# Four-layer graph network on one core: layer 0 and layer 2 sum the normed inputs, weights go to the sums or into the gates, x and out lie partition-major, and the first loads come in another order

## The chip, the cores and the metric

The kernel runs on one core of a Trainium2 chip. The metric is device time in microseconds (us), the median of several runs. One execution was taken by the hardware profiler; its page and its trace are what the text calls the profile. Engines: PE is TensorE (matmuls; PEld its weight loads), DVE is VectorE, ACT is ScalarE, POOL is GpSimd, SP is SyncE.

## The reference, cut to what matters

The input x has 4096 rows of 64 numbers, adj is a 4096 x 4096 matrix of zeros and ones (0.8% ones). Each of four layers norms x per row, applies relu, runs a graph operation with adj, and adds the result to x.

```python
h = relu(layernorm(x))
# layer 0: w is a matrix of decaying powers of 0.5, from a running count of each row's ones
x = x + (w @ (h @ L0_weight) + L0_bias)
# layer 1: attention, masked by adj, on Lorentz-projected h; then x = x + support / norm
# layer 2: two gated steps, each
m = adj @ (g @ W)
gi = m @ wih.T + bih
gh = g @ whh.T + bhh
r = sigmoid(i_r + h_r); z = sigmoid(i_z + h_z); n = tanh(i_n + r * h_n)
g = relu((1 - z) * n + z * g)
# layer 3: weighted midpoint in hyperbolic space: adj @ (gamma * XW), adj @ (gamma - 1), row sums
```

Since matrix products associate, `w @ (h @ W)` is `(w @ h) @ W`, and `(adj @ (g @ W)) @ wih.T` is `(adj @ g) @ (W @ wih.T)`. The change uses both.

## The kernel before, in words

Rows are kept in 32 blocks of 128; block b, partition p, is row 128 b + p. Four quarters of 8 blocks (`q`) are the unit of most vector work: a tile of 128 partitions x 8 blocks x 64 features, 512 numbers to a partition. The adjacency is read once, transposed, as 128 tiles of 128 x 1024 numbers (quarter of columns q, block of rows b), and cast to fp8 on the way by GpSimd's queue (`load0`, L1084 to L1089); it stays on the chip. The same matrix is read a second time as it is, in 128 f32 tiles named `whole`, by the sync queue (`checks`, L1049), only to check that every entry is 0 or 1; VectorE does that in whatever gaps it has. A flag from it chooses a general path, which isn't taken here.

Layer 0 (`stream0`, L1091) walks over the tiles. For each, matmuls with two triangular matrices (`ftri`, `fupd`) keep a running count in PSUM (`cnt`); ScalarE or VectorE turns the count into a power of two (`w`), and two steps later `sums` multiplies `w` with the source. A source in f32 is split by `split3` into three bf16 parts, `hm` (two parts, 128 columns) and `lo` (one, 64 columns), so that bf16 matmuls add up to f32 accuracy. Before the change the source is `h @ w0`: `pre0` norms a quarter of x (`relu_ln`), transposes it on PE (`transpose4`, tile `ps_t`), multiplies it by the weights (`linear4`, tile `ps_l`) and splits. After the sums of a quarter, `post0` takes them from PSUM (`evac`), adds the bias there, transposes them back (`to_nm`, tile `ps_n`), adds them to x and goes on to `pre1`, the projections of layer 1.

Layer 1 (`stream1`) computes scores, a sigmoid, a mask and f32 sums. Then `post1` ends with `source2`: transpose the normed input g, send the transposed copy to memory (`g_spill`), multiply it by W (`linear4`), split. Layer 2 (`layer2`, two steps) sums fp8 adj with these sources; `load2` brings the spilled copy back beside the sums; `gates` multiplies sums and copy by the gate weights in one matmul of 128 rows (64 for the sums, 64 for the copy), four gate columns per parity of the column block; `post2a` makes the second step's source from the result, again with `source2`. Layer 3 (`layer3`) sums a 196-column source, and `post3` writes out.

Nothing of this order is left to the hardware. A planner (`Weave`) runs when the program is built: it keeps a clock for each engine from estimated costs, and a piece of vector work (a generator) is put into the program where its estimated start fits. `weave.work` is served first, two pieces at a time (`width`), `weave.back` (the checks) last. `land` estimates when a transfer arrives, one after another at 1.45 us for an adjacency tile. `until` puts pending work into the program until a named source is done. Each engine then runs its own list in order, and a wait stops what stands behind it.

At the start, the sync queue loads four quarters of x, ScalarE's queue the constants W (553 KB), and GpSimd first builds the identity and an index pattern, then loads A tiles. x is loaded a second time in layer 0, quarter by quarter, for the residual sum. In memory x is by rows, so a quarter comes in pieces of 64 numbers (256 B); so does out.

Of the kernel before, what the change touches and what calls it, by code (L numbers as in the profile page):

```python
# [18 lines left out]
P = 128  # L19
# [16 lines left out]
def general_kernel(ctx: ExitStack, tc: tile.TileContext, t: dict, out: bass.AP):  # L36
# [50 lines left out]
    x_nm = t["x"].rearrange("(b p) d -> p b d", p=P)  # L87
# [438 lines left out]
    out_nm = out.rearrange("(b p) d -> p b d", p=P)  # L526
# [54 lines left out]
class Layout:  # L581


    def __init__(self):
        self.n = 0
        self.at = {}
        for name, width in (("w0", 2 * D), ("w1", 2 * D), ("wkq", 4 * D), ("gw1", 2 * D), ("gw2", 2 * D),
                            ("w3", 2 * D), ("b1", D), ("bkq", 2 * D), ("b0", 1), ("gb1", 6), ("gb2", 6),
                            ("scales", 5), ("g1", 8 * D), ("g2", 8 * D)):
            self.at[name] = slice(self.n, self.n + width)  # L590
            self.n += width
# [200 lines left out]
def fast_kernel(ctx: ExitStack, tc: tile.TileContext, t: dict, out: bass.AP, flag: bass.AP):  # L792
# [47 lines left out]

    W = const.tile([P, L.at["scales"].stop], F32, name="W")
    x_nm = t["x"].rearrange("(b p) d -> p b d", p=P)
    xq = {}

    def load_x(q):
        xq[q] = b2(f"x{q}")
        Y_.dma_start(xq[q], x_nm[:, q * QB:(q + 1) * QB, :])
        weave.at[xq[q].tensor.name] = 6.0 + 1.0 * (NQ - 1 - q), "S"

    for q in range(NQ)[::-1]:  # L850
        load_x(q)
    S_.dma_start(W, t["consts"][:, :L.at["scales"].stop])
# [17 lines left out]
    S_.activation(es, w("scales", 0, 3), AF.Exp)  # L870
    att_mul = const.tile([P, 1], F32, name="fatt_mul")
    V.reciprocal(att_mul, w("scales", 4, 5))
    V.tensor_scalar(att_mul, att_mul, 2.0, None, op0=ALU.mult)
    att_add = const.tile([P, 1], F32, name="fatt_add")
    V.tensor_tensor(att_add, att_mul, w("scales", 3, 4), ALU.add)
    gate_b = const.tile([P, 4], F32, name="gate_b")
    for i in (1, 2):
        V.tensor_tensor(gate_b[:, 2 * i - 2:2 * i], w(f"gb{i}", 0, 2), w(f"gb{i}", 3, 5), ALU.add)


    A8 = [[const.tile([P, 2, 2 * CW], F8, name=f"A{q}_{i}") for i in range(NB // 2)] for q in range(NQ)]
# [5 lines left out]
    def squares(v, nb=QB):  # L887

        sq = b2("sq")[:, :nb, :v.shape[2]]
        yield AC.activation(sq, v, AF.Square)  # L890
        s = stat("ss", nb)
        yield DV.tensor_reduce(s, sq, AX.X, ALU.add)
        return s
# [23 lines left out]
    def relu_ln(x, dst):  # L917

        m = stat("mean", QB)
        yield DV.tensor_reduce(m, x, AX.X, ALU.add)  # L920
        xc = b2("xc")
        yield DV.scalar_tensor_tensor(xc, rows(m), -1.0 / D, x, op0=ALU.mult, op1=ALU.add)
        v = yield from squares(xc)
        yield DV.tensor_scalar(v, v, 1.0 / D, LN_EPS, op0=ALU.mult, op1=ALU.add)
        r = yield from rsqrt(v)
        yield DV.scalar_tensor_tensor(dst, xc, 0.0, rows(r), op0=ALU.max, op1=ALU.mult)
# [48 lines left out]
    def split3(ps, scale, hm, lo):  # L975

        yield AC.activation(hm[:, :, :D], ps, AF.Copy, scale=scale)
        r = b2("rest")
        yield DV.scalar_tensor_tensor(r, ps, scale, hm[:, :, :D], op0=ALU.mult, op1=ALU.subtract)
        free(ps)  # L980
        yield AC.activation(hm[:, :, D:], r, AF.Copy)
        yield DV.tensor_tensor(lo, r, hm[:, :, D:], ALU.subtract)
# [5 lines left out]
    def parts(layer, q):  # L988
        HM[layer, q] = b2(f"hm{layer}_{q}", (P, QB, 2 * D), BF16)
        LO[layer, q] = b1p.tile([P, QB, D], BF16, tag="b1", name=f"lo{layer}_{q}")  # L990
        return HM[layer, q], LO[layer, q]
# [4 lines left out]
    def add_hm(acc, layer, b, c, rhs, first, last=False):  # L996
        o = like(acc[c], rhs)
        mm(o, HM[layer, b // QB][:, b % QB, :], rhs, start=first, stop=last)

    def add_lo(acc, layer, b, c, rhs, last):  # L1000
        o = like(acc[c], rhs)[c * D:(c + 1) * D]
        mm(o, LO[layer, b // QB][:, b % QB, :], rhs, start=False, stop=last)

    def evac(acc, bias=None):

        lo, hi = slice(0, D), slice(D, P)
        a, mt = b2("agg", (P, CW)), b2("mt", (P, CW))
        sides = ((lo, hi), (hi, lo))
        for ps, (own, other) in zip(acc, sides):
            yield AC.activation(mt[own, :], ps[other, :], AF.Copy)  # L1010
        for ps, (own, other) in zip(acc, sides):
            if bias is None:
                yield DV.tensor_tensor(a[own, :], ps[own, :], mt[own, :], ALU.add)
            else:
                yield DV.scalar_tensor_tensor(a[own, :], ps[own, :], bias[own, :], mt[own, :],
                                              op0=ALU.add, op1=ALU.add)
            free(ps)
        return a
# [17 lines left out]
    def pre0(q):  # L1036
        h = b2("h0")
        yield from relu_ln(xq[q], h)
        fm = b2("h0T", (P, CW))
        yield from transpose4(h, 1, fm)  # L1040
        yield from split3(blocks((yield from linear4(fm, w("w0"), 1))), W0, *parts(0, q))
        DONE.add((0, q))
# [39 lines left out]
    tiles = [(q, b) for q in range(NQ) for b in range(NB)[::-1]]  # L1082

    def load0(n):  # L1084

        if n < len(tiles):
            q, b = tiles[n]
            weave.land(A8[q][b // 2].tensor.name, 1.45)
            nc.gpsimd.dma_start(A8[q][b // 2][:, b % 2, :], adjT[b * P:(b + 1) * P, q * 2 * CW:(q + 1) * 2 * CW])  # L1089

    def stream0():  # L1091
# [4 lines left out]
        def turn(q, b):  # L1096

            n = q * NB + NB - 1 - b
            a = a8(q, b)
            wt = b2("w", (P, 2 * CW), I16)  # L1100
            for c in (0, 1):
                if b < NB - 1:
                    before = a8(q, b + 1)(c)
                    mm(like(cnt[c], before), upd, before, start=False, stop=False)
                mm(like(cnt[c], a(c)), tri, a(c), start=b == NB - 1, stop=b == 0)

                if c == 0 or b % 2 == 0:
                    S_.activation(wt[:, cols[c]], cnt[c], AF.Relu, scale=-128.0)
                else:
                    V.tensor_scalar(wt[:, cols[c]], cnt[c], -128.0, 0.0, op0=ALU.mult, op1=ALU.max)  # L1110
            load0(n + 12)
            return [wt[:, x].bitcast(BF16) for x in cols]
# [20 lines left out]
        def here(item):  # L1133
            part = 0, item[1] // QB
            return part in DONE and weave.ready("P", names(LO[part])) <= weave.t["P"]

        for q in range(NQ):
            cnt[:] = [two(f"cnt{c}")[:, :CW] for c in (0, 1)]
            for b in range(1, NB, 2)[::-1]:

                if len(waiting) > 3:
                    weave.until((0, waiting[0][1] // QB), DONE)
# [11 lines left out]
                waiting.append((q, b, w0, w1))  # L1154
                if len(waiting) > 2 and here(waiting[0]):
                    for _ in sums():
                        weave.draw()
                if b == NB // 2 + 1:
                    xq[q] = b2(f"x{q}")
                    Y_.dma_start(xq[q], x_nm[:, q * QB:(q + 1) * QB, :])  # L1160
# [15 lines left out]
    def post0(q, acc):  # L1176
        X = xq.pop(q)
        a = yield from evac(acc, w("b0"))
        ps = yield from to_nm(a, 1)
# [146 lines left out]
    def post1(q, acc, kind):  # L1326
# [20 lines left out]
        yield from relu_ln(X[q], g)  # L1347
        gT = b2("gT", (P, CW))
        yield from transpose4(g, kind, gT)
        yield from source2(q, 0, gT, kind)  # L1350
# [4 lines left out]
    def source2(q, step, gT, kind):  # L1355
        g_spill[step, q] = dram.tile([P, CW], F32, name=f"gs{step}_{q}")
        yield AC.dma_start(g_spill[step, q], gT)
        ps = yield from linear4(gT, w(f"gw{step + 1}"), kind)
        yield from split3(blocks(ps), 1.0, *parts(2 + step, q))
        DONE.add((2 + step, q))  # L1360
# [36 lines left out]
    def layer2(step, post):  # L1397
# [11 lines left out]
        for q in range(NQ):  # L1409
            load2(step, q)  # L1410
# [19 lines left out]

    def gates(q, step):
# [4 lines left out]
        rz, ih = [None], [None]  # L1436

# [26 lines left out]
    def post2a(q):  # L1464
        x = yield from gates(q, 0)
        yield AC.activation(x, x, AF.Relu)
        yield from source2(q, 1, x, 1 if q < NQ - 1 else 2)
# [108 lines left out]
    out_nm = out.rearrange("(b p) d -> p b d", p=P)  # L1576
# [59 lines left out]
    out_nm = out.rearrange("(b p) d -> p b d", p=P)  # L1636
# [66 lines left out]
    weave.dma = 5.2  # L1703
    for n in range(12):
        load0(n)
    for q in range(NQ)[::-1]:
        weave.add(pre0(q))
# [4 lines left out]
    gate_w = []  # L1712
    for step in range(2):
        gate_w.append(b2(f"g{step}", (P, 8 * D)))
        Y_.dma_start(gate_w[step], t["consts"][:, L.at[f"g{step + 1}"]])
# [5 lines left out]
def pack_consts(given):  # L1721
# [20 lines left out]
    for r in (0, D):  # L1742
        put("b0", given("L0_gnn_bias").reshape(D, 1), r)
    for i, name in enumerate(("scale", "scale_q", "scale_k", "att_bias", "att_scale")):
        put("scales", np.broadcast_to(given("L1_gnn_" + name).reshape(1, 1), (P, 1)), 0, i)
    for i in (1, 2):
        diag(f"gw{i}", given(f"L2_gnn_W{i}"))
        ih, hh = given(f"L2_gnn_wih{i}").T, given(f"L2_gnn_whh{i}").T
        for par in range(2):
            x, m = (0, D) if par == 0 else (D, 0)  # L1750
            for g, (wm, wx) in enumerate(((0, 0), (1, 1), (None, 2), (2, None))):
                col = (4 * par + g) * D
                if wm is not None:
                    put(f"g{i}", ih[:, wm * D:(wm + 1) * D], m, col)
                if wx is not None:
                    put(f"g{i}", hh[:, wx * D:(wx + 1) * D], x, col)
# [52 lines left out]
```

## Time and profile before

| | |
|---|---|
| Time, median of 3 runs | 824.69 us (824.64 to 824.71) |
| Span of the profiled run | 823.2 us |
| PE, DVE, ACT, POOL busy | 786.9, 625.3, 398.0, 69.8 us |
| First matmul starts | 7.97 us |
| First sum of layer 0 (`acc`) | 21.98 us |
| First score of layer 1 | 239.88 us |
| Last matmul ends | 802.5 us |
| DMA packets, of these under 512 B | 56,499 and 17,648 |

Busy is the time in which an engine had work in hand; matmuls are pipelined, so a busy PE is not PE at its peak. The chain of work that ended last is followed back from the last instruction, at each step to what released it. A wait is put down to the engine or transfer that came last.

### The profile page before, as it was taken

How to read it: one execution, taken by the hardware profiler on the slowest of the kernel's cores; microseconds unless marked ns; L12 is line 12 of the kernel's file. 1: busy time of each engine (PE TensorE's matmuls, PEld its weight loads, DVE VectorE, ACT ScalarE, POOL GpSimd, SP SyncE). 2: the span in 40 equal slices, each digit the busy share in tenths (PEclk: the TensorE clock that was granted, in tenths of full speed). 3: DMA queues.
4: the chain of work that ended last, by engine and by line, in shares of the span. 5: the costliest groups of instructions: out<-in, count | busy, mean ns of one | idle time of the engine just before them, and what ended most of it. 6: DMA issues, size and time to landing. Idle time of an engine off the chain costs nothing.

```text
span 823.2 us, 12224 instructions
## 1 busy us (share of the span) xinstructions
PE 786.9 (96%) x4570; PEld 367.6 (45%) x4570; DVE 625.3 (76%) x1393; ACT 398.0 (48%) x607; POOL 69.8 (8%) x143
## 2 busy tenths in 40 slices
PE   5989999999999999999999999999999999999990
PEld 2433444443433333333333333444444444699990
DVE  6565666676567888888888878978789787775896
ACT  5646556556565567666666663022210244452323
POOL 4322324323000000000000000000000000000000
PEclk9999999999999999999999999999999999999995
DMA  9999999999901023022022025796879900000010
GB/s 134 113 235 221 156 220 115 175 200 156 203 21 40 1 91 114 1 89 65 1 89 65 1 70 198 270 340 214 277 248 349 322 15 14 1 2 2 2 40 17
DMA packets 56499, 100.54 MB, mean 122 GB/s; under 512 B 17648, under 2 KB 34032, under 8 KB 56432
## 3 DMA queue, kind: packets, MB, share of 16 engines
q1 hardware_dynamic: 36128, 79.18, 29.1%
q0 software_dynamic: 18432, 16.79, 21.7%
q10 hardware_dynamic: 1872, 3.71, 1.2%
q8 instruction: 38, 0.62, 0.3%
q14 instruction: 29, 0.24, 0.1%
HBM read 144.75 MB, written 5.24 MB: 182 GB/s over the span
## 4 chain that ended last, share of the span: by engine, by line
PE 86%; DVE 7%; DMA 3%; ACT 2%; issue 1%; SPq 0%; POOL 0%; DVEq 0%; ACTq 0%; POOLq 0%
PE acc L940 52%; PE score L940 13%; PE cnt L940 12%; DMA whole<-in_adjT 3%; PE ps_l L940 2%; PE rz L940 2%; DVE sig L781 2%; PE ps_t L944 2%; PE ih L940 1%; DMA A<-in_adjT 1%; DVE ss L781 1%; PE ps_kq L940 1%; DVE nt L781 1%; ACT sig L781 1%; PE ps_n L944 0%
## 5 line engine op out<-in xcount | busy, mean ns | idle before, releaser
L781 ACT ACTIVATE sig<-score,fatt_add,fatt_mul 128x1024 f32<-128x1024 f32 x128 | 148.0, 1201 | 83.0 <-PE score L940 80.8
L781 DVE TENSOR_TENSOR sig<-sig,A 128x1024 f32<-128x1024 f32 x128 | 151.4, 1222 | 35.9 <-ACT sig L781 35.2
L781 DVE SCALAR_TENSOR_TENSOR whole<-whole 128x1024 f32<-128x1024 f32 x128 | 153.1, 1219 | 9.5 <-DMA whole<-in_adjT 8.7
L781 ACT ACTIVATE w<-cnt 128x512 int16<-128x512 f32 x192 | 108.4, 595 | 91.4 <-PE cnt L940 90.2
L940 PE MATMUL score<-qd,kT 64*128 64x512 f32 x512 | 128.0, 616 | 0.0
L940 PE MATMUL acc<-sig,S 128*64 128x512 f32 x512 | 125.4, 606 | 1.7 <-DVE sig L781 1.6
L940 PE MATMUL acc<-A,hm 128*128 128x512 fp8e4 x512 | 115.9, 379 | 0.8 <-DVE X L781 0.8
L940 PEld LDWEIGHTS <-hm 128*128 128x128 bf16 x768 | 73.2, 98 | 91.1 <-issue 12.6
L940 PE MATMUL cnt<-A,ftri 128*128 128x512 fp8e4 x256 | 97.8, 385 | 8.0 <-DMA A<-in_adjT 8.0
L940 PE MATMUL cnt<-A,fupd 128*128 128x512 fp8e4 x248 | 95.4, 385 | 4.6 <-DVE w L781 3.0
L940 PE MATMUL acc<-S,A 128*128 128x196 bf16 x1024 | 88.3, 247 | 0.0
L940 PEld LDWEIGHTS <-A 128*128 128x128 fp8e4 x1024 | 87.2, 97 | 1.1 <-issue 0.8
L781 DVE TENSOR_SCALAR w<-cnt 128x512 int16<-128x512 f32 x64 | 44.2, 691 | 54.7 <-PE cnt L940 51.5
L1089 POOL DMA_DIRECT2D A<-in_adjT x128 | 68.0, 533 | 141.4 <-DMA A<-in_adjT 136.9
L940 PEld LDWEIGHTS score<-qd,kT 64*128 64x128 f32 x512 | 43.8, 186 | 79.8 <-ACT sig L781 35.3
L940 PE MATMUL acc<-w,hm 128*128 128x512 bf16 x256 | 75.5, 379 | 0.0
L940 PEld LDWEIGHTS acc<-sig,S 128*64 128x64 f32 x512 | 30.4, 136 | 81.1 <-issue 38.5
L940 PEld LDWEIGHTS <-lo 128*64 128x64 bf16 x768 | 36.8, 109 | 58.2 <-issue 36.5
L940 PE MATMUL acc<-A,lo 128*64 128x512 fp8e4 x512 | 59.3, 380 | 0.0
L781 ACT ACTIVATE mt<-acc 64x512 f32<-64x512 f32 x32 | 18.9, 592 | 64.7 <-PE acc L940 64.1
L1565 POOL MEMSET S<- 128x4 bf16 x8 | 0.9, 116 | 529.3 <-PE ps_l L940 484.0
L940 PEld LDWEIGHTS <-fupd 128*128 128x128 bf16 x248 | 24.3, 98 | 44.5 <-issue 22.3
(176 smaller groups left out, 652.8 us busy)
## 6 DMA issues: line engine op xcount, KB each, us to landing
whole<-in_adjT SPq DMA_DIRECT2D x128, 512.0 KB, 6.8
A<-in_adjT POOLq DMA_DIRECT2D x128, 128.0 KB, 12.4
x<-in_x SPq DMA_DIRECT2D x8, 256.0 KB, 15.5
qd<-qs SPq DMA_DIRECT2D x16, 128.0 KB, 4.5
mx<-gs SPq DMA_DIRECT2D x16, 128.0 KB, 8.1
xT<-gs SPq DMA_DIRECT2D x8, 256.0 KB, 7.5
xs<-x SPq DMA_DIRECT2D x4, 256.0 KB, 5.9
qs<-qT ACTq DMA_DIRECT2D x4, 256.0 KB, 6.1
```

Of the source, the lines that this page charges most:

```text
L781: return fn(*args, **kw)
L940: nc.tensor.matmul(o, lhsT, rhs, start=start, stop=stop, skip_group_check=True)
L944: nc.tensor.transpose(o, src, ident)
L1089: nc.gpsimd.dma_start(A8[q][b // 2][:, b % 2, :], adjT[b * P:(b + 1) * P, q * 2 * CW:(q + 1) * 2 * CW])
L1565: nc.gpsimd.memset(S3[q, c][:, :, 3 * e:], 1.0)
```

## The change

The change does four things. Layer 0 takes `h` itself as source; `post0` multiplies the sums by `w0` (`linear4` in place of `to_nm`), and the bias is added to x. Layer 2 takes g itself as source; its W is multiplied into the gate weights on the chip, once per step (`load_gates`: one f32 matmul of 192 columns, four copies into the gate matrix), and the transposed copy is spilled after the split. x and out lie in memory as partition x block x feature, arranged on the host, so that a quarter is 2 KB to a partition. And the first loads are reordered: A, x, A, x ahead of the identity; quarters 1 and 0 of x and the constants during the stream, the last on ScalarE's queue; the last quarter's first norm in two halves; its vector work and that of the next quarter on VectorE alone, and the first 12 tiles' `w` on ScalarE alone. It is meant to take matmuls off TensorE and to start the stream earlier.

```diff
-    x_nm = t["x"].rearrange("(b p) d -> p b d", p=P)
+    x_nm = t["x"]
...
-    for q in range(NQ)[::-1]:
-        load_x(q)
-    S_.dma_start(W, t["consts"][:, :L.at["scales"].stop])
+    weave.dma = 1.0
+    load0(0)
+    load_x(3, Y_)
+    load0(1)
+    load_x(2, Y_)
...
-    def pre0(q):
-        h = b2("h0")
-        yield from relu_ln(xq[q], h)
-        fm = b2("h0T", (P, CW))
-        yield from transpose4(h, 1, fm)
-        yield from split3(blocks((yield from linear4(fm, w("w0"), 1))), W0, *parts(0, q))
-        DONE.add((0, q))
+    def pre0(q, c=None):
+        x = xq[q] if c is None else xq[q][:, c * CB:(c + 1) * CB]
+        h = b2("h0")[:, :x.shape[1]]
+        dve = q > 1
+        yield from relu_ln(x, h, dve)
+        yield from split3(h, W0, *parts(0, q, c), psum=False, dve=dve)
+        DONE.add((0, q) if c is None else (0, q, c))
...
-                if c == 0 or b % 2 == 0:
+                if c == 0 or b % 2 == 0 or n < 12:
                     S_.activation(wt[:, cols[c]], cnt[c], AF.Relu, scale=-128.0)
...
+                if q == 0 and b in (NB - 1, NB - 3):
+                    load_x((b - NB + 3) // 2, S_)
+                    weave.add(pre0((b - NB + 3) // 2))
+                if q == 0 and b == NB - 9:
+                    S_.dma_start(W, t["consts"][:, :L.at["scales"].stop])
+                    weave.add(constants())
...
-        a = yield from evac(acc, w("b0"))
-        ps = yield from to_nm(a, 1)
+        yield DV.tensor_tensor(X, X, w("b0")[:, None, :].to_broadcast([P, QB, D]), ALU.add)
+        a = yield from evac(acc)
+        ps = blocks((yield from linear4(a, w("w0"), 1)))
...
+        yield from split3(g, 1.0, *parts(2, q), psum=False)
+        DONE.add((2, q))
         gT = b2("gT", (P, CW))
         yield from transpose4(g, kind, gT)
-        yield from source2(q, 0, gT, kind)
+        yield from spill2(q, 0, gT)
...
-        ps = yield from linear4(gT, w(f"gw{step + 1}"), kind)
-        yield from split3(blocks(ps), 1.0, *parts(2 + step, q))
-        DONE.add((2 + step, q))
+        DONE.add(("spill", step, q))
...
+    def load_gates(step):
+
+        g, m = b2(f"g{step}", (P, 8 * D)), b2(f"m{step}", (P, 5 * D))
...
+            ps = two("ps_g")
+            mm(ps[:, :3 * D], m[:, :2 * D], m[:, 2 * D:])
...
-        yield from source2(q, 1, x, 1 if q < NQ - 1 else 2)
+        ps = yield from to_nm(x, 1 if q < NQ - 1 else 2)
+        yield from split3(ps, 1.0, *parts(3, q))
+        DONE.add((3, q))
+        yield from spill2(q, 1, x)
...
-    for q in range(NQ)[::-1]:
-        weave.add(pre0(q))
+    for c in (1, 0):
+        weave.add(pre0(NQ - 1, c))
+    weave.add(pre0(NQ - 2))
```

## The prediction, made before the change was run

> **What bounds the kernel now.** I read the page's busy times and the chain first, then the groups, then 5 us stretches and the timeline of the first 25 us, then TensorE's waits. The page:
>
> ```profile
> PE 786.9 (96%) x4570; PEld 367.6 (45%) x4570; DVE 625.3 (76%) x1393; ACT 398.0 (48%) x607; POOL 69.8 (8%) x143
> ...
> PE 86%; DVE 7%; DMA 3%; ACT 2%; issue 1%; SPq 0%; POOL 0%; DVEq 0%; ACTq 0%; POOLq 0%
> ```
>
> TensorE (PE) is 86% of the chain that ended last, and its idle time is 823.2 - 786.9 = 36 us. Most of that lies at the ends: 8 us before the first matmul, and 21 us after the last (802.5 to 823.2), where VectorE works through layer 3's last sums. So a matmul taken away between 22 and 800 us should show in the end, and one put in should cost. The stretches of the start say where else PE idles (columns: length, then PE, PEld, DVE, ACT, POOL busy, clock, DMA share, GB/s):
>
> ```profile
> 0.00:5.00 5.00, 0.00 (x0) 0.10 (x1) 0.72 (x3) 1.28 (x1) 4.39 (x14) 1.00 0.57 173
> 5.00:10.00 5.00, 1.77 (x4) 0.51 (x4) 4.32 (x17) 1.43 (x3) 1.71 (x4) 1.00 1.16 137
> ...
> 45.00:50.00 5.00, 4.13 (x24) 2.04 (x23) 1.88 (x4) 2.58 (x6) 1.06 (x2) 1.00 1.08 254
> 50.00:55.00 5.00, 3.62 (x22) 1.67 (x21) 3.64 (x6) 2.28 (x4) 1.06 (x2) 1.00 1.08 256
> ```
>
> The DMA engines are full from 5 us on (share above 1), and there is a hole of 2.3 us between 45 and 55 us. PE's waits in the first 60 us:
>
> ```profile
> PE cnt L940 <- DMA A<-in_adjT: 8.0, 1, 8.0
> PE cnt L940 <- DVE w L781: 2.8, 3, 1.5
> PE cnt L940 <- ACT w L781: 0.8, 3, 0.3
> ```
>
> The first wait is for the first adjacency tile, which shares the DMA engines with four loads of x and 553 KB of constants. The second is VectorE stuck on a check of the adjacency (`whole`) whose transfer, issued at 30.6, was queued behind a load of x and landed only at 47.4. The rows that I price with:
>
> ```profile
> L940 PE MATMUL ps_l<-W,h0T 128*128 128x128 f32 x32 | 4.2, 275 | 0.0
> L944 PE MATMUL ps_n<-fident,agg 128*128 128x128 f32 x32 | 5.0, 280 | 0.0
> L940 PE MATMUL ps_kq<-W,hlT 128*128 128x256 f32 x32 | 8.4, 386 | 0.0
> x<-in_x SPq DMA_DIRECT2D x8, 256.0 KB, 15.5
> A<-in_adjT POOLq DMA_DIRECT2D x128, 128.0 KB, 12.4
> ```
>
> Means of pipelined matmuls overlap, so I take a group's cost from the chain, where a piece runs to the next start: four transposes 0.44 us, one `linear4` 0.89 us (1.09 where it follows the half-array matmuls of layer 1).
>
> [...] `cnt` matmuls start at 9.62, 10.05, 10.47, then from 13.08 every 0.215 us. About 10 cold matmuls cost 10 x 0.21 = 2.1 us[...]. [...] x in rows of 64 floats is 256 B, 1024 packets a load, and its median landing is 15.5 us, while a 512 KB `whole` tile takes 6.8. [...] DMA shares above 1 agree that the engines are the limit. [...] the trace has 20 at 1283.
>
> **Part by part.**
>
> (a) Layer 0 sums `h` and not `h @ w0`. `pre0` loses four transposes and a `linear4`: 4 x (0.44 + 0.89) = 5.3 us of PE, and a ScalarE copy (0.59) each. `post0` pays for it: `linear4` in place of `to_nm`, 4 x (0.89 - 0.44) = +1.8 us. The bias becomes one VectorE add of 0.69 us per quarter on x, issued before the sums are evacuated, so it lies beside the end of the sums: zero. Net PE -3.5 us.
>
> (b) Layer 2, first step: `linear4` goes. On the chain its four read 1.09, 1.09, 1.09 and 0.89, so -4.2 us. The first three lie inside layer 1, which PE bounds (10.0 busy of each 10 us from 300 to 480). The fourth is on the 12 us way from the last `ps_n` (505) to the source of the last quarter; PE has the sums of other blocks there, so only its own time counts.
>
> (c) Layer 2, second step: `linear4` becomes four transposes, 3.8 - 2.0 = -1.8 us. The spill to memory now follows the split in place of leading it, and the reload waits for it; the reload of quarter 0 comes after the source of quarter 3 is done, some 20 us later, and the mx and xT loads land in 8 us. Hidden by the block sums.
>
> (d) Weights folded on the chip: one f32 matmul of 192 columns per step, by the 256-column row (0.43 us a matmul in the chain) 0.33 each, +0.65 us, plus four short ScalarE copies of half height and 160 KB of extra load each, beside PE. They need a two-bank PSUM tile, which at 500 us is free. Bounds 0.4 to 1.5; I take 0.7.
>
> (e) First loads. The first A tile goes out ahead of everything, with only one x load beside it. Before, it was issued at 1.46 and the first matmul came at 7.97. Lower bound of the new landing: issue at about 0.5 plus 3.7 (the shortest landing of a 512 KB tile) = 4.2; upper bound: 0.5 plus 6.5, the shortest A landing so far, = 7.0. The triangle matrices are ready at 2.3 now and perhaps 3.3 after, so they hide. I take 5.0: -3 us. Will PE then have work? Tiles arrive every 1.25 to 1.45 us (spacing of the POOL issues, without and with x beside them); a cold tile costs 4 x 0.43 = 1.7, so supply holds through the warm-up. The sums begin when the split of the last blocks is done: x lands at about 4, then 8 VectorE operations on 256 elements (0.42) and 9 small ones (0.2) make 5.2 us, so 9.5 to 12 us, where before the first sum stood at 21.98. From then PE has 3.25 us of work for each pair of tiles against 2.9 at most of supply.
>
> All of it on VectorE is three chains, 5.2 + 5.2 + 7.5 = 18 us in the first 22, which is why `w` goes to ScalarE alone for 12 tiles: 1.2 us a tile, less than the supply takes. It fits, narrowly.
>
> (f) Constants come mid-stream: the Exp now needs a table load at about 20 us, 1.28 us of ScalarE while PE waits for its `w`. Bounds 0 and 1.3; I take +0.6.
>
> (g) x and out by partition: 2 KB pieces for 256 B. In layer 0 a load of x holds the A spacing at 1.45 for some 10 us where it is 1.25 without, and `whole` tiles queue behind it on the sync queue. I expect half of the 5 us of waits described below to go: -2.5. At the end the last store issues at 817.75 and the span ends 5.4 us later; fewer packets may save 0.3.
>
> **The sum.** Layer 0 up to the first score (239.9 us): 64 pairs of `cnt` at 1.83, 62 of sums at 1.42, 5.3 of `pre0` and 3 x 4.8 of `post0` and `pre1` are 225 us; the other 15 are 8 of start, 2 cold, 5 of waits. After: 225 - 5.3 + 3 x 0.45 = 221; lost 5.0 + 2.1 + 1 (until the sums run) + 2.5 + 0.6 = 11.2; together 232.2, so -7.7. The fourth `linear4` of `post0` stands in layer 1: +0.45. Layer 2: -4.2 - 1.8 + 0.7 = -5.3. End: -0.3. Total -12.8: 824.7 - 12.8 = 811.9, say 812.
>
> **The rivals.**
> Work only: the first tile lands hardly earlier, or the VectorE chains delay the sums, and a new wait replaces the old ones. Then (a) to (d) remain, about -9, less 1 for (f): 816.5. For it: the full DMA and VectorE's 18 us in 22.
> More: the hole at 45 to 55 us and the later waits on `w` go wholly, since no x blocks the queue, and the tile lands at 4.2: 2.5 + 1 + 0.8 more: 807.5. For it: all those waits trace to slow transfers.
> Slower: the schedule is planned from costs, and a shorter layer 0 holds fewer checks (10 us less at 1.4 each, some 8). They go to layer 2, where VectorE is full in several stretches (5.00 of 5 from 525), and what is left is put in one run ahead of layer 3's evacuations, which free PSUM: 8 x 2 us = 16, against 12.8 gained: 828. Against it: VectorE has 10 us of 15 free at 750 to 765.
> No change: the same with half that pile, 824.
>
> **How the numbers follow.** Forecast 0.58, work only 0.2, more 0.12, no change 0.04, slower 0.06. The range 806.5 to 818.5 takes in the first three with (d) to (g) at their bounds. Faster 0.90, same 0.04, slower 0.06.
>
> **What would show it.** First matmul at 4.2 to 7; first `acc` sum at 10 to 14; first score near 232; no `ps_l` from gT or xT; `ps_l` from agg in place of one `ps_n`; packets under 512 B down from 17,648 by the 8 x 1024 of x and the 4096 of out, to some 5,400; PE busy down by about 8 us. The forecast fails if PE shows a new wait on `w` in the first 25 us, if `whole` tiles stand in the last 60 us before the end with PE idle, or if A tiles come late between 25 and 80 us.

## The result, and the profile after

| | before | after |
|---|---|---|
| Time, median | 824.7 us (824.64 to 825.05) | 832.87 us (830.46 to 833.05) |
| Ratio, 95% interval | | 1.0091 (1.0073 to 1.011) |
| Span of the profiled run | 823.2 us | 831.3 us |
| First matmul, first sum of layer 0 | 7.97, 21.98 us | 7.10, 14.66 us |
| Last matmul ends | 802.5 us | 797.7 us |
| Packets under 512 B | 17,648 | 5,392 |

The change made the kernel slower by 0.9%, where 1.5% faster was forecast. The profiled run is the longest of the four. The page of the changed kernel, busy times and chain:

```profile
PE 780.2 (94%) x4494; PEld 358.9 (43%) x4494; DVE 629.2 (76%) x1415; ACT 396.7 (48%) x611; POOL 69.7 (8%) x143
...
PE 83%; DVE 8%; DMA 5%; issue 1%; ACT 1%; POOL 0%; DVEq 0%; ACTq 0%; POOLq 0%
```

TensorE (PE) has 6.7 us less to do, nearly the 8 forecast, and its last matmul ends 4.8 us earlier. Yet the span ends 8.1 us later: the tail behind the last matmul grew from 20.7 to 33.6 us, and the chain lies 8% on VectorE (DVE) in place of 7% of a shorter span. Cut by stage, from the first and last instruction of each group of matmuls (the last column is a run told below):

| us | before | forecast | after | both causes mended |
|---|---|---|---|---|
| start to first score | 239.8 | 232.2 | 234.3 | 234.2 |
| first to last score (layer 1) | 257.5 | 254.7 | 258.4 | 254.8 |
| last score to first layer-3 sum | 210.8 | 208.8 | 208.7 | 206.8 |
| first layer-3 sum to end | 115.1 | 114.8 | 129.9 | 116.3 |
| sum | 823.2 | 810.5 | 831.3 | 812.1 |

The forecast column takes the prediction's terms into their stages: 257.5 + 0.45 - 3 x 1.09, and 210.8 - 0.89 - 1.8 + 0.7. Layer 2 came out as forecast. Three stages did not, the last of them by 15 us. Each column is one profile. In the first row a difference of 1 us means little: the changed kernel's start is the same in nine of the runs told below, and there its first matmul stands at 6.1 to 6.9 us and not at 7.10, its first sum at 13.4 to 13.9 and not at 14.66; in the four of them that have the same layer 0 too, the first score comes at 233.1 to 233.6. VectorE's timeline of the changed kernel there (start, length, engine, line, operation, and in brackets the idle time before it and what ended it):

```profile
757.99 0.89 DVE L781 TENSOR_TENSOR n<-n,acc 128x260 f32<-128x260 f32 x2 [2.21 <-ACT alpha L781]
758.79 1.22 DVE L781 SCALAR_TENSOR_TENSOR whole<-whole 128x1024 f32<-128x1024 f32 x1
...
771.97 1.23 DVE L781 SCALAR_TENSOR_TENSOR whole<-whole 128x1024 f32<-128x1024 f32 x1 [0.61 <-DMA whole<-in_adjT]
...
773.23 1.23 DVE L781 SCALAR_TENSOR_TENSOR whole<-whole 128x1024 f32<-128x1024 f32 x1
...
774.78 0.62 DVE L781 TENSOR_TENSOR n<-n,acc 128x130 f32<-128x130 f32 x2
```

Between two pieces of layer 3's work on the sums stand twelve checks of the adjacency (`whole`), from 758.79 to 774.50, three of the last four waiting for their loads too (1.3 us together). They are the checks that found no gap in the earlier layers; `layer3` issues all that are left in one run, behind the sums of its second set. Before the change one check stood there. The tile `whole` from 740 us on, in the kernel before and in the changed one:

```profile
L781 DVE SCALAR_TENSOR_TENSOR whole<-whole x1: 1218/1218/1218, 765.5 to 765.5; 128x1024 f32<-128x1024 f32 x1
```
```profile
L781 DVE SCALAR_TENSOR_TENSOR whole<-whole x12: 1217/1218/1226, 758.8 to 773.2; 128x1024 f32<-128x1024 f32 x12
```

Stretches of the kernel before around its one check (columns: length, then PE, PEld, DVE, ACT, POOL busy, clock, DMA share, GB/s):

```profile
750.00:755.00 5.00, 5.00 (x62) 5.00 (x60) 0.88 (x3) 0.50 (x2) 0.00 (x0) 1.00 0.00 0
755.00:760.00 5.00, 5.00 (x62) 5.00 (x60) 1.16 (x4) 0.68 (x4) 0.00 (x0) 1.00 0.02 3
760.00:765.00 5.00, 5.00 (x61) 5.00 (x60) 1.48 (x5) 1.13 (x6) 0.00 (x0) 1.00 0.00 0
765.00:770.00 5.00, 5.00 (x61) 4.80 (x59) 4.76 (x17) 0.80 (x3) 0.00 (x0) 1.00 0.01 3
770.00:780.00 10.00, 10.00 (x121) 10.00 (x119) 9.14 (x46) 4.32 (x14) 0.00 (x0) 1.00 0.01 2
```

and of the changed kernel around the run and behind it:

```profile
745.00:750.00 5.00, 5.00 (x62) 5.00 (x60) 0.00 (x0) 0.00 (x0) 0.00 (x0) 1.00 0.00 0
750.00:755.00 5.00, 5.00 (x61) 5.00 (x60) 1.75 (x6) 1.24 (x8) 0.00 (x0) 1.00 0.00 0
755.00:758.80 3.80, 3.80 (x47) 3.80 (x46) 1.36 (x5) 0.57 (x4) 0.00 (x0) 1.00 0.02 4
758.80:774.50 15.70, 14.98 (x177) 14.75 (x174) 14.26 (x26) 1.02 (x6) 0.00 (x0) 1.00 0.60 202
...
780.00:790.00 10.00, 10.00 (x121) 10.00 (x119) 8.78 (x40) 3.31 (x9) 0.00 (x0) 1.00 0.00 0
...
800.00:810.00 10.00, 0.00 (x0) 0.00 (x0) 9.17 (x46) 5.12 (x9) 0.00 (x0) 0.59 0.01 2
810.00:820.00 10.00, 0.00 (x0) 0.00 (x0) 9.11 (x44) 4.18 (x9) 0.00 (x0) 0.50 0.13 45
```

VectorE is nearly idle ahead of the checks in both kernels, and this idle time isn't used by them. In the changed kernel the loads of the first six had landed by 682.2 us, and VectorE was idle for 11.2 us between 744 and 758; yet the first check starts at 758.79. VectorE takes its list in order, and what stands in front of the checks are the evacuations, which take layer 3's sums out of PSUM. Each waits for ScalarE's part of the same evacuation (`alpha`), and ScalarE for TensorE's sums (2.4 us before the last of them, the one at 757.99). The other six checks were loaded only from 760.0 on, when the first gave their buffers back. Behind the checks VectorE has few gaps (before 4.76 of 5, then 9.1 to 9.3 of 10 up to 800 and 8.6 up to 810; after 8.4 to 9.2 of 10 from 780 to 820), so the run moves what follows by about its own length. It is 14.4 us longer than the one check was, and the stage 14.8. TensorE waited once for VectorE to empty a PSUM bank (`acc` on `sgn`, 1.8 us), and the other 13 us stand behind the last matmul.

The start, in the stretches that the prediction shows of before, and from 35 to 45 us, where TensorE was full before (5.00 of 5):

```profile
0.00:5.00 5.00, 0.00 (x0) 0.10 (x1) 1.59 (x9) 1.28 (x1) 3.90 (x13) 1.00 0.58 120
5.00:10.00 5.00, 2.64 (x6) 0.80 (x6) 4.45 (x18) 1.67 (x3) 2.53 (x6) 1.00 1.07 94
...
35.00:40.00 5.00, 3.43 (x17) 1.18 (x16) 1.20 (x3) 2.01 (x4) 1.06 (x2) 1.00 1.08 252
40.00:45.00 5.00, 4.09 (x21) 1.55 (x20) 2.59 (x8) 2.96 (x7) 1.51 (x3) 1.00 1.11 152
45.00:50.00 5.00, 5.00 (x27) 1.79 (x26) 3.50 (x13) 2.77 (x5) 2.10 (x5) 1.00 1.12 106
50.00:55.00 5.00, 5.00 (x26) 2.02 (x24) 3.40 (x6) 3.32 (x6) 2.09 (x5) 1.00 1.12 105
```
```profile
PE cnt L954 <- DMA A<-in_adjT: 9.9, 5, 7.1
PE cnt L954 <- ACT w L781: 0.4, 2, 0.3
```

The hole at 45 to 55 us is gone with the wait on VectorE's `w`; but a new one stands at 33 to 43. The second fence, the waits of the first 60 us, names it: five waits for A tiles in place of one, the first of 7.1 us and four more of 2.8 together. Four A tiles in turn come 2.6 us apart there, beside five `whole` loads of 512 KB. The sync queue issues these at 22.5 to 24.4 us now (before from 30.6), and the x load ahead of them on it lands in 6.6 us, not in 14.7. That they make the A tiles late is read from the times; no run held them back.

### The profile page after: what moved, and what is told of

Read it like the earlier page. It is cut to its first block, busy times and chain, and to the rows that moved or that the text cites. A ratio compares the mean times of both kernels' runs of the same rounds, so it can differ in the third digit from the quotient of the medians.

```text
span 831.3 us, 12127 instructions
## 1 busy us (share of the span) xinstructions
PE 780.2 (94%) x4494; PEld 358.9 (43%) x4494; DVE 629.2 (76%) x1415; ACT 396.7 (48%) x611; POOL 69.7 (8%) x143
## 2 busy tenths in 40 slices
DMA packets 46546, 100.75 MB, mean 121 GB/s; under 512 B 5392, under 2 KB 23056, under 8 KB 46480
## 4 chain that ended last, share of the span: by engine, by line
PE 83%; DVE 8%; DMA 5%; issue 1%; ACT 1%; POOL 0%; DVEq 0%; ACTq 0%; POOLq 0%
PE acc L954 50%; PE score L954 14%; PE cnt L954 12%; DMA A<-in_adjT 4%; PE rz L954 2%; DVE sig L781 2%; PE ih L954 1%; PE ps_t L958 1%; PE ps_l L954 1%; DVE whole L781 1%; DVE ss L781 1%; DMA whole<-in_adjT 1%; PE ps_kq L954 1%; DVE n L781 1%; DVE nt L781 1%
## 5 line engine op out<-in xcount | busy, mean ns | idle before, releaser
L781 ACT ACTIVATE w<-cnt 128x512 int16<-128x512 f32 x198 | 111.1, 595 | 97.8 <-PE cnt L954 96.3
L781 DVE SCALAR_TENSOR_TENSOR whole<-whole 128x1024 f32<-128x1024 f32 x128 | 153.0, 1219 | 5.9 <-DMA whole<-in_adjT 4.8
L954 PE MATMUL score<-qd,kT 64*128 64x512 f32 x512 | 129.9, 624 | 0.0
L781 DVE TENSOR_SCALAR w<-cnt 128x512 int16<-128x512 f32 x58 | 40.1, 691 | 66.9 <-PE cnt L954 63.1
```

The lines of the kernel that those rows point to most:

```text
L781: return fn(*args, **kw)
L954: nc.tensor.matmul(o, lhsT, rhs, start=start, stop=stop, skip_group_check=True)
```

## The experiments

Two sets of numbers are read in each run: the stages of the table above, and how many of the 128 checks stand in layers 0, 1, 2 and in the last run, counted in VectorE's list of instructions (before 33, 38, 56, 1; after 26, 36, 54, 12). For this count layer 1 ends with the first sums taken out in layer 2, some 40 us after the last score. Three theories were named: PILE, the last run of checks makes the loss; STALLS, the new waits of TensorE make it; STORE, the end comes late from the new way of storing. All ratios are to the kernel before.

**The last run of checks.** Leave the 12 checks and their loads out of the changed kernel (the entries they cover are then not checked):

```diff
-        todo = [(b, c) for c in range(NQ) for b in range(NB)]
+        todo = [(b, c) for c in range(NQ) for b in range(NB)][:116]
```


> The changed kernel without its last 12 checks of the adjacency (their loads and VectorE operations are left out, so 12 of 128 tiles go unchecked). Theory PILE: the loss is the run of 12 checks at 758.8 to 774.5, ahead of layer 3's evacuations; without it the last matmul ends near 796, the stretch after it is again near 21 us instead of 33.6, and the time is 816 to 820. Rival STALLS: the loss is the new waits of TensorE before 300 us (2.8 us for A tiles, the slow stretch at 290 to 300); then 831 to 833, since nothing before 640 us changes. Rival STORE: the partition-major stores at the end are slower; also 831 to 833.

Measured: 815.38 us, ratio 0.9875 (0.9858 to 0.9891). The last stage takes 113.4 us, 16.5 less; the other stages stand within 1.2 us of the changed kernel's. The store is the new one, and the waits in layers 0 and 1 are still there.

The other way round, the kernel before with a pile: with `lead` at 0 the planner takes fewer checks into layer 0 (19 for 33), and 15 are left.

```diff
-    lead = [13]
+    lead = [0]
```


> The kernel before, with the loads of checks in layer 0 held back (the lead of the DMA clock over TensorE's from 13 to 0), which leaves 15 checks in one run ahead of layer 3's evacuations in place of 1; nothing of the change is in it. PILE: 836 to 842, the loss of the changed kernel and more without any of its edits. STALLS and STORE: 820 to 825, a little faster if anything, since fewer checks compete in layer 0.

Measured: 852.97 us, 1.0335 (1.0318 to 1.0353). The last stage takes 144.2 us, 29 more than before, with the old store and none of the changed sources. A pile alone slows the old kernel, and by 11 us more than the 842 allowed: the run itself is 18 us longer than one check; TensorE waits 5.3 us for it (`sgn`), the longest `acc` matmul of layer 3 takes 369 ns (258 before), the mean granted clock of the run is 0.973 (0.989), and then one VectorE instruction (`sq`) waits 7.0 us for the sums that have become late.

The changed kernel with `lead` at 20, so that 39 checks stand in layer 0 and none is left:

> The changed kernel with more checks let into layer 0 (lead 13 to 20: 39 checks there in place of 26, none left at the end). PILE: no run at the end, 816 to 824, of which up to 6 us may go to later A tiles in layer 0. STALLS: slower than the changed kernel, 834 to 842, as waits for A tiles grow with 13 more transfers of 1.3 us. STORE: 831 to 833 and the waits on top.

Measured: 820.72 us, 0.9941 (0.9925 to 0.9958). The last stage falls to 113.3, but the first score comes at 240.4, 6.1 us later: 13 more checks in layer 0 are not free. TensorE waits there for VectorE's `w` (2.3 us, 0.2 in the changed kernel) and 10.7 us for A tiles (9.9); these make 2.9 of the 6.1, the rest stays open.

The changed kernel with one check put behind each sum of the second set, in place of the run:

```diff
                 sum3(u, place, lo * QB, hi * QB)
+                if weave.back and weave.back[0][1].e == "D":
+                    weave.issue(weave.back[0])
```


> The changed kernel with the same 128 checks, but one is put into the program after each partial sum of layer 3's second set of columns, so that no run of them stands on VectorE. PILE: 817 to 823, the work is the same and only its place is other; the checks ahead of the last source may cost 1 to 3 us. STALLS and STORE: 831 to 833.

Measured: 820.37 us, 0.9943 (0.9926 to 0.9959). The last stage takes 119.2 us. TensorE's wait moved: it now waits 4.0 us for the last source (`S`), whose making stands behind the checks on VectorE. Spreading saves most, but the same VectorE time is still in the stage.

PILE holds in both directions, STALLS and STORE fall for the bulk: in these runs and in the next ones the last stage grows with the number of checks left, in either kernel, 113.3 us at none, 115.1 at one, 118.6 at four, 120.4 at six, 129.9 at twelve, 144.2 at fifteen. It doesn't grow in proportion, and one run below has 124.2 with a single check, for another reason.

**One part at a time.** The kernel before with x and out partition-major alone:

> The kernel before with one part of the change alone: x and out partition-major. The planner's order is the same, one check is left at the end. If the waits on w in layer 0 came from slow loads of x, as the prediction had it, they shrink and the time is 821 to 823.5; if the planned order holds the waits whatever the loads do, 824 to 825.5.

Measured: 824.72 us, 0.9996 (0.9988 to 1.0005). TensorE's waits on VectorE's `w` fall from 3.0 to 0.7 us in all, as wanted; the first wait for an A tile grows by nearly as much (the first 60 us):

```profile
PE cnt L940 <- DMA A<-in_adjT: 9.9, 1, 9.9
PE cnt L940 <- DVE w L781: 0.5, 1, 0.5
```

The x loads issued in the first 30 us land after a median of 6.7 us (11.1 before), and the first A tile beside them comes 1.9 us later than before. The last stage takes 115.0 us with the new store, and 115.1 before.

The kernel before with layer 2's part alone:

> The kernel before with the layer 2 part alone (g as source, W multiplied into the gates). It leaves 4 checks in a run at the end in place of 1. By the matmuls taken out, minus 5.3; a run of 4 checks fits in VectorE's idle stretch ahead of the evacuations and costs 0 to 3: 819 to 823. If each check at the end costs its share of what 11 more cost (some 1.2 us): 823 to 825. If matmuls taken out of layers 1 and 2 are not on the path: 825 or more.

Measured: 822.81 us, 0.9974 (0.9965 to 0.9984). Layer 1 takes 254.1 us, 3.4 less: the three `linear4` removed. The stage after it is 2.1 shorter. Four checks are left for the end, which takes 118.6, 3.5 more, and eats most of it: 1.2 us for each further check.

Layers 0 and 2 and the layout, but the old order of the first loads:

> The change without its new order of first loads: layer 0 and layer 2 folds and the layout on the kernel before; x and the constants are loaded first, norms in whole quarters, no table load in mid-stream. 6 checks are left at the end. If the early start is worth the 3 to 6 us that the prediction gave it, the first score comes at 236 to 238 (before 239.9, changed 234.3); if layer 0 is held by the supply of A tiles and checks and not by the start, at 233 to 235. The time with 6 checks in a run: 818 to 824.

Measured: 823.24 us, 0.9982 (0.9975 to 0.9989). First score 235.4, between the two ranges, so the new first loads are worth 1.1 of the 5.5 us in layer 0 (2 us against the runs with 233.1 to 233.6). They cost more than that: six checks are left here and twelve with them, four of the six lost in layer 0 and two in layer 2, and the end takes 120.4 us here and 129.9 with them. Of the change's parts it is the new order of loads that turns a small gain into the loss, 9.6 us in all. Why it leaves so few checks a place stays open. Layer 1 takes 258.2 us although layer 2's part takes 3.4 from it: something gives 4 us back.

Layer 0's part alone (here the bias's tile is 64 columns wide, and the pool of small tiles is 20 deep, not 22, to make room for it):

> The kernel before with layer 0's part alone (h as source, linear4 on the sums, bias added to x), no new loads, no layout, layer 2 as before; 4 checks are left for the last run. PILE and SLOT: first score about 235.5 (4.3 earlier), of which layer 1 gives back 3.5 to 4 (first to last score 261.5 and not 257.5), the last stretch is 118.6 and not 115.1: in all slower than before, 826 to 828. Without the give-back in layer 1: 823 to 824. By the forecast's own sum (5.3 less, 1.8 more, of it 0.45 in layer 1): 820 to 821.

Measured: 827.65 us, 1.0033 (1.0025 to 1.0041): slower, though it takes 3.5 us of work from TensorE. First score 236.2, layer 1 260.0 (2.5 more), end 118.5 with four checks (3.4 more). Both losses are in this part; 0.45 us in layer 1 is the fourth `linear4`, which was forecast.

**The give-back in layer 1.** Stretches of the changed kernel in the first pass of layer 1, and the matmuls that move: the last quarter's `linear4` in the changed kernel, and `ps_n`, which stood in its place before (count, ns, first and last start). The keys of that quarter (`k`) follow from them.

```profile
288.00:290.00 2.00, 1.90 (x8) 0.20 (x4) 2.00 (x3) 1.28 (x2) 0.00 (x0) 1.00 0.07 12
290.00:292.00 2.00, 0.26 (x2) 0.26 (x3) 2.00 (x4) 0.00 (x0) 0.00 (x0) 1.00 0.72 244
292.00:294.00 2.00, 1.97 (x10) 0.99 (x10) 2.00 (x4) 1.20 (x2) 0.00 (x0) 0.80 0.06 14
294.00:296.00 2.00, 2.00 (x8) 0.69 (x4) 0.64 (x2) 0.88 (x1) 0.00 (x0) 0.50 0.52 115
296.00:298.00 2.00, 2.00 (x8) 0.48 (x8) 1.23 (x1) 1.51 (x2) 0.00 (x0) 0.85 0.69 266
```
```profile
L954 PE MATMUL ps_l<-W,agg x8: 275/275/377, 246.2 to 247.1; 128*128 128x128 f32 x8
```
```profile
L944 PE MATMUL ps_n<-fident,agg x4: 272/273/329, 248.6 to 248.9; 128*128 128x128 f32 x4
```

TensorE is idle for 1.8 us at 290 to 292, waiting for `k` from VectorE, and then runs at a granted clock (the share of its full clock that it is given) of 0.8, 0.5 and 0.85 for three stretches of 2 us, which by this share loses 0.4 + 1.0 + 0.3 = 1.7 us more: 3.5 together. The last quarter's sums start their last matmul at 239.0 and `linear4` comes 7.2 us later; in the kernel before, `ps_n` followed the sums' last matmul (244.5) after 4.1. An iteration of layer 1 is 3.8 us: the planner put it one iteration later. What stood new ahead of it was the bias add on x, first in `post0`. Moved behind `linear4`, nothing else, all 12 checks still in the last run:

```diff
-        yield DV.tensor_tensor(X, X, w("b0")[:, None, :].to_broadcast([P, QB, D]), ALU.add)
         a = yield from evac(acc)
         ps = blocks((yield from linear4(a, w("w0"), 1)))
+        yield DV.tensor_tensor(X, X, w("b0")[:, None, :].to_broadcast([P, QB, D]), ALU.add)
```


> The changed kernel with one instruction of post0 moved: the bias is added to x after the matmuls of linear4 and not before the sums are evacuated. All 12 checks stay in the last run. SLOT (the bias add ahead of the evacuation makes the planner put the last quarter's linear4 one iteration later, and its keys then come late in layer 1): linear4 of the last quarter comes about 3.8 us after the last sum and not 7, TensorE's wait for k (1.8) goes, first score to last score 255 and not 258.4, and with the pile unchanged 829 to 830. FIXED PLACE (the keys' transposes are put at the same iteration anyway, so the slot doesn't matter): no change, 832 to 833.

Measured: 828.34 us, 1.0041 (1.003 to 1.0051), 4.5 us below the changed kernel, of which 3.5 lie in layer 1 and 1.0 ahead of the first score, where the profiles differ anyway. The wait for `k` is gone, layer 1 takes 254.9 us, and

```profile
L954 PE MATMUL ps_l<-W,agg x8: 275/275/377, 242.1 to 243.0; 128*128 128x128 f32 x8
```

stands 4.1 us behind the last sum (238.0). SLOT is shown.

An earlier try at both losses forced the last keys one iteration sooner and raised the planner's allowance for vector work in layer 1 (`weave.late`, how far a piece may end behind TensorE's clock) from 1.0 to 1.7:

```diff
-                if q == 0 and i % (QB // 2) == 0:
-                    weave.until((1, i // (QB // 2)), DONE)
+                if q == 0 and i % (QB // 2) == QB // 2 - 1 and i < NB // 2 - 1:
+                    weave.until((1, (i + 1) // (QB // 2)), DONE)
...
-                weave.late = 2.0 if weave.quiet else 1.0
+                weave.late = 2.0 if weave.quiet else 1.7
```


> The changed kernel with two edits to the planner: checks may end up to 1.7 us after the moment (1.0 before) in layer 1, so that 46 fit there in place of 36 and 1 is left at the end; and the keys of the next quarter are asked for one iteration earlier in layer 1's first pass, so that the last quarter's chain on VectorE goes ahead of four masks. PILE alone: 815 to 817. With the wait in layer 1 gone as well, 811 to 815. If more checks in layer 1 push masks back, 817 to 822.

Measured: 818.57 us, 0.9914 (0.9897 to 0.9931). One check is left (116.3 us at the end), but the wait for `k` grew to 3.7 us and layer 1 to 260.2: forcing the use sooner does nothing for a chain that is late. The allowance alone:

> The changed kernel with the planner's allowance for vector work in layer 1 raised from 1.0 to 1.7 us, nothing else: 45 checks fit into layer 1 in place of 36 and 2 are left for the run ahead of layer 3's evacuations, in place of 12. PILE: layer 0 and layer 1 as in the changed kernel (first score 234.3, last 492.7), the stretch from the first layer-3 sum to the end falls from 129.9 to 116 to 117, time 819 to 820. If the nine checks more in layer 1 get into TensorE's way there, the last score comes later than 494 and the time is 822 or more.

Measured: 818.7 us, 0.9918 (0.9896 to 0.9939); nine checks more in layer 1 cost nothing there (258.6 us), the wait for `k` stays at 1.8. Two checks are left, and the end takes 117.6.

**Both mended.** The bias moved and the allowance at 1.6, one check left:

> The changed kernel with both: the bias add after linear4, and the allowance in layer 1 raised to 1.6, which leaves 1 check in the last run; all 128 checks are done. PILE and SLOT: first score 234, layer 1 in 255, last stretch 115 to 116, time 813 to 815, the 12 us that were forecast for the change. PILE without SLOT: 817 to 818.5.

Measured: 822.32 us, 0.9963 (0.9949 to 0.9976), a miss of 8. Layer 1 was right (255.3). The end takes 124.2 us with its one check. The longest of TensorE's waits from 690 to 800 us was

```profile
PE acc L954 <- DVE S L781: 5.4, 1, 5.4
```

The planner had put the last quarter's gate matmuls (`rz`) behind 240 matmuls of layer 3, where the run with the allowance alone had 64, so the last source (`S`) came late. Two more settings keep the gates early. With the allowance at 1.9, no check left, gates behind 48:

> The changed kernel with the bias add after linear4 and the allowance in layer 1 at 1.9: no check is left for the last run, and the last quarter's gates stand behind 48 layer-3 sums. If the two causes are the whole miss: first score 233 to 234, layer 1 in 255 to 257 (13 more checks on VectorE there may cost some), first layer-3 sum 696 to 698, last stretch 113 to 115, no wait for S of 5 us, time 811 to 814. If something else is left: 818 or more.

Measured: 816.15 us, 0.9894 (0.9878 to 0.9911), a miss of 2. The end takes 113.4 us, layer 1 255.5; but TensorE waits 2.8 us for ScalarE's `r` in the gates, and the stage between is 213.0. With the allowance at 1.7 and `lead` at 15, one check left, gates behind 64:

> The changed kernel with the bias add after linear4, the allowance in layer 1 at 1.7 and two checks more ahead of the stream in layer 0: 1 check is left for the last run, and the last gates stand behind 64 layer-3 sums, the one placement that differs from the run that gave 822.3. If that placement made its miss: first score 234 to 235, layer 1 in 255, no wait for S, last stretch 115 to 117, time 813 to 816. If not: 820 to 823 again.

Measured: 813.86 us, 0.9872 (0.9856 to 0.9889): the best kernel of the study, all 128 checks done, 19.0 us below the changed kernel and 10.9 below the one before. It differs from the run of 822.3 in the allowance (1.7 for 1.6) and in `lead`; the place of the gates is what its expectation turned on, and the wait for `S` is gone. Its last stretches:

```profile
770.00:780.00 10.00, 10.00 (x120) 10.00 (x119) 9.48 (x36) 2.12 (x7) 0.00 (x0) 1.00 0.13 42
780.00:790.00 10.00, 10.00 (x121) 10.00 (x119) 9.09 (x46) 5.36 (x13) 0.00 (x0) 1.00 0.01 5
790.00:800.00 10.00, 2.18 (x26) 1.95 (x23) 8.82 (x44) 4.28 (x12) 0.00 (x0) 0.87 0.12 40
800.00:810.00 10.00, 0.00 (x0) 0.00 (x0) 5.61 (x31) 2.06 (x5) 0.00 (x0) 0.50 0.09 30
```

VectorE is as full as in the kernel before, TensorE doesn't idle in these stretches until its last matmul at 792, and the end comes 19 us sooner than in the changed kernel.

## Why the prediction was wrong

It went the way of the rival called "Slower" (828), which had been given 0.06. Of the 20.8 us by which the span missed the forecast, 15.1 lie in the last stage, 3.7 in layer 1 and 2.1 at the start. **The step that failed** is the argument against that rival, by which the sum put the left-over checks at nothing: "VectorE has 10 us of 15 free at 750 to 765". The free time was there (11.5 of 15 by the lines shown), and it lay ahead of the place where the checks stand: the one check at 765.5 in the profile before was followed by a nearly full VectorE, and the evacuations at 757 to 764 it stood behind were waiting for sums. Free time in front of a waiting instruction is no use to what is queued behind it: the last stage took 129.9 us, 14.8 more than before. The number was short as well: "some 8" came from layer 0 alone; it was 7 there, 2 in layer 1 and 2 in layer 2, 11 in all, at 14.8 / 11 = 1.3 us each, where the rival had 8 at 2 us. That its 828 comes near is in part luck, then: more checks at a lower price, on top of losses in layer 1 and at the start that it didn't have. "No change" was mis-summed: half of 16 us on 811.9 is 820, not 824. Two of the prediction's own three signs of failure came: A tiles late between 25 and 80 us, and `whole` tiles near the end with TensorE idle (the last two of them inside the last 60 us). A rival whose mechanism follows of itself from the forecast (a shorter layer 0 must hold fewer checks) needs a count, not a small chance.

(a) Layer 0's fold: the TensorE work is right; "the bias add lies beside the end of the sums: zero" is wrong. The time of the add isn't the cost (0.69 us for the one at 239.02); with it ahead of the evacuation the planner put `linear4` one iteration later: 1.8 us of wait and 1.7 of clock in layer 1. With the bias moved, layer 1 takes 254.9 us where the forecast's terms give 254.7.

(b) to (d) Layer 2: right. 3.4 us in layer 1 (forecast 3.3) and 2.1 in the stage after (2.0).

(e), (f), (g) The start: the first sum came 7.3 us earlier, but the first score only 5.5 (6.2 to 6.7 in the four other runs with this layer 0; forecast 7.7). The first matmul stood at 7.10, just beyond the bound of 7.0, in the nine other runs with these loads at 6.1 to 6.9, never at 5.0; and the 2.5 us of waits on `w` that (g) counted did go, for 2.8 us of waits on A tiles between 33 and 42 us. The order of the loads is worth 1 to 2 us in layer 0, and its six checks cost 9.5 at the end. The table load of (f) didn't come: both kernels have 20 (`ACT_TABLE_LOAD`, 1283 ns each), none of them between 3 and 90 us, and the Exp stands at 43.11 us and takes 0.21. So (f) was 0 and not +0.6. The A tiles came later beside longer pieces: in the run with the layout alone, with pieces of x of 2 KB for 256 B, TensorE waited 9.9 us for the first A tile and not 8.0; and beside `whole` loads (pieces of 4 KB) the A tiles came 2.6 us apart in both kernels (from 49 to 77 us in the one before), and not 1.25 to 1.45 as earlier in that kernel, without and with x beside them. That the length of the pieces makes it was not shown: no run changed it for one queue alone in mid-stream.

What would have shown it before the run: VectorE's timeline at 757 to 775, with the one left check between waiting evacuations and 55 us in which VectorE has few gaps. A kernel whose last filler just fits has no slack for the next.

The rest of the sum was near: with the pile and the slot out of the way, and with two settings of the planner raised for it, the kernel takes 813.9 where 812 was said. The start is 2.0 us longer than forecast, layer 1 0.1, and the last two stages together 0.5 shorter.

## What to carry to other kernels

When filler work is planned into gaps, a change that shortens a stage removes gaps; count how many pieces lose their place and find where the leftovers go, before adding up the gain. Count it for each part of a change: here a part worth 1 to 2 us in its own stage left six pieces over and cost 9.5 us at the end. Idle time on an engine that works in order helps only what stands ahead of the instruction that waits; what is queued behind it, with a full engine after it, goes straight to the end (here twelve checks stood behind 11.2 us of idle time, and the last stage grew by 14.8 us). In an order that is fixed ahead, a cheap instruction in front of a chain can cost a whole iteration (here an add of 0.69 us cost 3.5 us in layer 1): look at the slot of the chain's next step, not at the duration of the addition.

## What the runs showed of the hardware that was not expected

An idle time of 1.8 us cost nearly its length again in clock. After it, in layer 1, the granted clock of the changed kernel fell to 0.5; by the shares above this took 1.7 us more. With the bias moved the wait went, the clock stood at 1.00 from 290 to 300 us, and layer 1 became 3.5 us shorter. It isn't sure to happen. Seven profiles have this same wait of 1.8 us for `k`: in five the longest `score` matmul then takes 1133 to 1219 ns, and in four of these the stretches show the same 1.7 us of clock lost; in two it takes 693 ns, as in the kernel before. One of the two is the run with the checks spread over layer 3, whose VectorE, ScalarE and TensorE work through the changed kernel's list, instruction for instruction, up to there; its layer 1 takes 256.8 us where the changed kernel's takes 258.4. So the program alone didn't decide it. The other is layer 0's part alone, at a clock of 1.00 before and after,

```profile
292.00:294.00 2.00, 0.32 (x3) 0.32 (x4) 2.00 (x4) 0.00 (x0) 0.00 (x0) 1.00 0.73 242
294.00:296.00 2.00, 1.97 (x14) 1.02 (x13) 2.00 (x4) 1.20 (x2) 0.00 (x0) 1.00 0.05 14
```

and the 1.8 us for `sgn` in the changed kernel's layer 3 left it at 1.00 too. What decides it was not shown.
